# A two-layer graph attention kernel: weight loads tied to ScalarE during the scores, a reordered softmax at the end of a pass, and block stores moved to the second superblock

## The chip, the cores and the metric

The kernel runs on one core of one Trainium2 chip. The metric is the device time of one execution in microseconds (us); the figure given for a kernel is the median of several executions. A core has a matrix engine (TensorE, PE in the profile), three engines for element-wise work (VectorE, DVE; ScalarE, ACT; GpSimd, POOL) and a queue engine (SyncE, SP) that issues nearly all transfers here. Every engine runs its own instructions in order and waits for the others by semaphores.

## The reference, cut to what matters

The input is x, 128 graphs of 64 nodes with 768 features, and a symmetric adjacency of zeros and ones for each graph. A layer norm and a rectifier give h; two graph attention layers follow; x is added at the end.

```python
h = jnp.maximum(_layernorm(x, axis=-1), 0.0)
for l in range(L):                                             # L = 2
    m_left  = jnp.einsum('bsh,oh->bso', h, W_left[l])
    m_right = jnp.einsum('bsh,oh->bso', h, W_right[l])
    u_left  = jnp.einsum('bih,bjh->bij', h, m_left) / temper
    u_right = jnp.einsum('bih,bjh->bij', h, m_right) / temper
    u = u_left * adj_tri + u_left * diag_mask + u_right * jnp.swapaxes(adj_tri, 1, 2)
    delta_exp_u = jnp.exp(u) * adj
    attention = delta_exp_u / (jnp.sum(delta_exp_u, axis=2, keepdims=True) + 1e-10)
    h_lin = jnp.einsum('bsh,oh->bso', h, W_lin[l]) + b_lin[l]
    h = jax.nn.relu(_layer_norm(jnp.matmul(attention, h_lin), ln_a[l], ln_b[l]))
return x + h
```

All arithmetic is in float32.

## The kernel before, in words

The graphs are cut into 16 blocks of 8 graphs (512 tokens), and for the first half of the work two blocks make a superblock: U = 0 to 7, of which U = 1 is "superblock two". Each layer has two passes.

**Pass one** (`pass_one`) computes, per superblock, the two projections `m_left` and `m_right` and, one superblock later, the scores and the softmax. The projections are not done as plain matrix products: the features are taken in three pairs of 128, and sums and differences of weight blocks (`W_OPS`) and of token blocks (`X_OPS`) turn the products into 29 smaller ones (`PRODUCTS`, NP = 29). `project` runs them: for product i, and for left and right (k = 0, 1), four calls of the matmul at line 522 into one of the PSUM banks X, Y, Z (left), V, `right` (right), and then `read`, in which ScalarE (line 303) or VectorE (line 221) adds a finished bank to the results `m`. At two fixed places, after products 0 and 2, `scores` (line 464) is put into the stream: 96 small matmuls for the first and for the second block of the superblock before. Each shows in the trace as 192 matmuls and as many weight loads of the array.

Order is written out by hand. A superblock has SLOTS = 116 slots, four to a product; `put(slot, f)` puts a piece of work there and `run(slot)`, called inside the loop over products, issues it; `idle` holds work that fills slots with nothing planned. So what stands in an engine's queue, and in which order, follows from slots, and each engine then waits only for what its instructions need.

**Weights.** In the first superblock of layer 0 (`first`) the sums of weights are computed on the way and each finished pair is stored to memory (`ws`, line 194). From then on `streamed` brings the pairs back: a ring of RINGS = 8 buffers `wp`, one 512 KB load per product (`stream`, line 197), sent by `done(i)`, which is called after product i:

```python
            HELD = {NP - 2: 1, NP - 1: 2, 0: 3, 1: 4}
                    while sent[0] < min(U * NP + i + RINGS - HELD.get(i, 0), NU * NP):
```

Without HELD, the load for product i + 7 is put into SP's queue after product i. With it, the loads that would stand around the two `scores` come later in the queue, all after product 2. The load itself waits only until the product that last used its buffer is finished on TensorE, wherever it stands in the queue.

**Tokens and h.** In layer 0, `load_rows` (line 368) brings a block's rows, `transpose_rows` computes mean and variance (line 338), the scale (394 to 396), the norm (399, ScalarE) and the transposes (414, VectorE), and `store` (410) puts the block's h into memory (`KEPT`, 1.5 MB); `load_h` (373) brings it back to the buffers `ht` when its turn comes. `block` places these steps in a superblock for the two blocks of the next one, from the slots in `starts`. Blocks 0 and 1 are made inside `first`, and their h is stored at slots 54 and 58 of superblock one (line 675) for use in pass two.

**Softmax.** `chain(u)` is a generator: masks (473, GpSimd), then as steps of `softmax(u)` the masked scores (480, two steps), their sum (484), the exponential (486, ScalarE), product and row sum (488, 490), division (492 to 494), a transpose (498) and eight small stores (504). Inside the pass these steps lie in slots. For the last two blocks, NB - 2 and NB - 1, they stand at the end of `pass_one`, lines 762 to 768, after their scores, with a part put into slots of pass two.

**Pass two** (`pass_two`) computes the third projection in `linear` (15 products of a similar scheme, line 1038, each read out by `read`), the product with the attention (`context`), the norm and the output. The bank X is set ahead of the first product by `fresh` (line 812); product 0 and product 2 both use bank X, so ScalarE must have read it between the two.

Of the kernel before, what the change touches and what calls it, by code (L numbers as in the profile page):

```python
# [17 lines left out]
def kernel(  # L18
# [12 lines left out]
    nc = tc.nc  # L31
# [25 lines left out]
    RINGS = 8  # L57
# [5 lines left out]
    none = [None]  # L63

    def put(slot, *fs):
        plan.setdefault(slot, []).extend(fs)

    def put_all(slot, fs, step=1):
        for f in fs:
            if f is not None:  # L70
                put(slot, f)
            slot += step
        return slot
# [50 lines left out]
    NP = len(PRODUCTS)  # L124
# [10 lines left out]
    RING = [wpool.tile([P, 2, K2, D], F32, name=f"wp{i}") for i in range(RINGS)]  # L135
# [4 lines left out]
    def room(n, m):  # L140
        return ROOM[:, n * K2 * D:(n + m) * K2 * D]
# [54 lines left out]
    def stream(l, n):  # L196
        nc.sync.dma_start(RING[n % RINGS], WS[l][n % NP])
# [34 lines left out]
    HT, TS = {}, {}  # L232
# [42 lines left out]
    def token_op(l, U, op, eng):  # L275
        i, o, sign, a, b = op
        t = new_ts((l, U, o))
        added(eng, t, sign, tokens(l, U, a), tokens(l, U, b))
        TS.setdefault((l, U), {})[o] = t

    AHEAD_X = 4
    SLOTS = 4 * NP

    def put_token_ops(l, U, part):

        count = {}
        for op in X_OPS:
            n = count[op[0]] = count.get(op[0], 0) + 1
            slot = 4 * (op[0] - AHEAD_X) + n - 1
            if (slot < 0) == (part == "before"):  # L290
                put(slot + (SLOTS if slot < 0 else 0), lambda op=op: token_op(l, U, op, nc.gpsimd))
# [20 lines left out]
    KEPT = [[dram.tile([P, C, T], F32, name=f"h{l}_{u}") for u in range(NB)] for l in range(L)]  # L312
# [4 lines left out]
    eps_in = const.tile([P, 1], F32, name="eps_in")  # L317
# [28 lines left out]
    def new_ht():  # L346
        turns.rotate(-1)
        return big.tile([P, C, T], F32, name=f"ht{turns[-1]}", bufs=1)
# [6 lines left out]
    def blocks_tile(pool):  # L355
        if pool is not None:
            return pool.tile([P, H // 32, Q, 32], F32, name="xb", bufs=1)
        return room(6, 6).rearrange("p (b q j) -> p b q j", q=Q, j=32)

    def load_rows(l, u, pool=None):  # L360

        XR[l, u] = []
        for g in range(2):
            t = rows_tile(pool, g)
            for a in range(4):
                i = 4 * g + a
                src = x[u * NBB + i] if l == 0 else ROWS[u][i]
                nc.sync.dma_start(t[a * 32:(a + 1) * 32], src.rearrange("(k j) h -> j k h", k=2))
            XR[l, u].extend([t[:, 0, :], t[:, 1, :]])
# [14 lines left out]
    def transpose_rows(l, u, pool=None):  # L384

        xr, todo = XR[l, u], []
        if l == 0:
            mv = stat.tile([P, Q, 2], F32, name="mv0", bufs=2)
            sd = stat.tile([P, Q], F32, name="sd0", bufs=2)
            rs = stat.tile([P, Q], F32, name="rs0", bufs=2)  # L390
            nb = stat.tile([P, Q], F32, name="nb0", bufs=2)

            def scale():
                nc.scalar.activation(sd, mv[:, :, 1], AF.Sqrt, bias=eps_in)
                nc.vector.reciprocal(rs, sd)
                nc.vector.scalar_tensor_tensor(nb, mv[:, :, 0], -1.0, rs, op0=ALU.mult, op1=ALU.mult)

            def norm(q):
                nc.scalar.activation(xr[q], xr[q], AF.Relu, bias=nb[:, q:q + 1], scale=rs[:, q:q + 1])

            norms = [lambda q=q: norm(q) for q in range(Q)]
            stats = [lambda q=q: mean_var(mv[:, q, :], [xr[q][:, :HH], xr[q][:, HH:]]) for q in range(Q)]
            for f in stats + none * (4 * (u < 4)) + [scale] + norms:
                todo.extend([f] + none * (u >= 4))
        xb = blocks_tile(pool)

        def store():
            to = KEPT[l][u].rearrange("(b i) c t -> i c b t", b=4)
            for a in range(4):
                nc.sync.dma_start(to[:, :, :, a * P:(a + 1) * P],  # L410
                                  xb[a * 32:(a + 1) * 32].rearrange("i (c b) q j -> i c b (q j)", b=4))

        for q in range(Q):
            todo.append(lambda q=q: nc.vector.transpose(
                xb[:, :, q, :], xr[q].rearrange("p (b j) -> p b j", j=32)))
            todo.extend(none * (l or u >= 4))
        todo.append(store)
        return todo
# [7 lines left out]
    def pass_one(l, aside):  # L426
        with (tc.tile_pool(name=f"ps_one{l}", bufs=1, space=bass.MemoryType.PSUM) as ps,
# [76 lines left out]
                        nc.sync.dma_start(to[a // 2, a % 2, g], at[a * 32:(a + 1) * 32, g])  # L504

            TURNS = {0: 0, 2: 1}
            HELD = {NP - 2: 1, NP - 1: 2, 0: 3, 1: 4}
            sent = [RINGS - 1 if l else NP + 5]

            def project(U, weights, done):  # L510
# [35 lines left out]
            def streamed(U):  # L546
                def done(i):
                    while sent[0] < min(U * NP + i + RINGS - HELD.get(i, 0), NU * NP):
                        stream(l, sent[0])
                        sent[0] += 1  # L550
                return (lambda i, k: RING[(U * NP + i) % RINGS][:, k]), done

            def first():
# [47 lines left out]
                hts = [new_ht() for _ in range(2)]  # L601
# [66 lines left out]
                for n, (s0, s1, s2, s3) in {4: (3, 4, 5, 8), 5: (6, 7, 8, 12), 6: (13, 14, 15, 19),  # L668
# [2 lines left out]
                    put(s1, lambda n=n: inverse(n))  # L671
                    put(s2, lambda n=n: norm(n))
                    put(s3, lambda n=n: turn(n), lambda n=n: settle(n))
                for n, slot in ((0, 54), (1, 58)):
                    put(slot, lambda n=n: nc.sync.dma_start(KEPT[0][n], hts[n]))
                put(3, lambda: load_rows(0, 2))
                count = {}
                for op in X_OPS:
                    n = count[op[0]] = count.get(op[0], 0) + 1
# [28 lines left out]
            for U in range(NU):  # L708
                if U:
                    weights, done = streamed(U)  # L710
                if l or U:
                    put_token_ops(l, U, "after")
                if U + 1 < NU:
                    def block(n, slot):
                        u = 2 * U + 2 + n
                        *todo, store = transpose_rows(l, u)
                        slot = put_all(slot, todo)
                        put(slot + 6, store)
                        if u + 1 < NB:
                            put(slot + 7, lambda: load_rows(l, u + 1))  # L720
                        slot = max(slot + 15, (92, 103)[n]) if U == 0 and l == 0 else slot + 15
                        put(slot, lambda: load_h(1, l, u))
                        if l:
                            put_all(slot + 20, affine(1, l, u))

                    if l:
                        starts = (6 if U else 20, 48)
                    else:
                        starts = (6, 52) if U else (26, 66)
                    for n, slot in enumerate(starts):  # L730
                        put(slot - 1, lambda n=n, slot=slot: block(n, slot))
                    if U:
                        for n in range(2):
                            steps = softmax(2 * U - 2 + n)
                            slot = put_all(20 + 40 * n if l else (34, 76)[n], steps[:6], 2)
                            slot = put_all(slot, steps[6:] + [lambda n=n: load_adj(2 * U + n)])
                            put(slot + 11, masked(2 * U + n))
                    else:
                        for n in range(2):
                            put((40 if l else 106) + 2 * n, masked(n))  # L740
                    put_token_ops(l, U + 1, "before")
                else:
                    for n in range(2):
                        put(12 + 28 * n, lambda n=n: load_h(2, l, n))
                        put_all(38 + 28 * n, affine(2, l, n))
                    for n in range(2):
                        steps = softmax(2 * U - 2 + n)
                        put_all(put_all(14 + 28 * n, steps[:6], 2), steps[6:])
                    put(40, lambda: load_adj(2 * U))
                    put(54, masked(2 * U))  # L750
                    put(SLOTS - 24, lambda: load_adj(2 * U + 1))
                    put(SLOTS - 10, masked(2 * U + 1))
                    put_sums_t((2, l, 0), 94, 2, 85)
                if U in aside:
                    aside[U]()
                project(U, weights, done)
                assert not plan, sorted(plan)
# [5 lines left out]
            scores(NB - 2, both[0])  # L763
            scores(NB - 1, ps_st.tile([P, 2 * TH], F32, name="Z"))
            one, two = softmax(NB - 2), softmax(NB - 1)
            for f in one[:2] + two[:2] + one[2:] + two[2:4]:
                f()
            put_all(2, two[4:])

    rows = {}  # L770

# [406 lines left out]
```

## Time and profile before

| | |
|---|---|
| median of 3 executions | 2746.46 us (2743.89 to 2749.26) |
| profiled execution | 2748.58 us |
| its span, first to last instruction | 2746.8 us |
| TensorE busy | 2689.4 us, 98% |
| VectorE, ScalarE, GpSimd busy | 54%, 30%, 50% |
| transfers | 567.81 MB, mean 207 GB/s |

Busy time is an average over stages. TensorE is busy nearly throughout, so what matters is where it is idle, and what it waits for there. In the lines of the profile, "out<-in xcount" names the buffers, the bracket at the end of a timeline row holds the idle time of the engine before it and what ended it, and "issue" is a wait for nothing that the profile shows. PE stands for the matmul, PEld for the load of the array's weights, L522 for line 522.

### The profile page before, as it was taken

The page shows a single profiled execution, that of the slowest core. Times are in us where ns is not written, and L with a number is a line of the kernel's source. Part 1 is how long each engine was busy: PE and PEld are TensorE (multiplying, and loading weights), DVE is VectorE, ACT ScalarE, POOL GpSimd, SP SyncE. Part 2 cuts the span into 40 slices and gives each one's busy share as a digit, 9 for nine tenths or more (in the row PEclk, how much of TensorE's full clock was granted, in tenths as well). Part 3 has the DMA queues.
Part 4 walks back from the last instruction along what each step waited for, and adds up shares of the span by engine and source line. Part 5 has one row for each costly group of instructions (what it writes and reads, how often), then busy time and mean ns, then how long its engine had stood idle before and what let it go on. Part 6 is the DMA issues. An engine that isn't in the chain of part 4 may idle for free.

```text
span 2746.8 us, 47294 instructions
## 1 busy us (share of the span) xinstructions
PE 2689.4 (98%) x18514; PEld 2309.1 (84%) x18514; DVE 1494.6 (54%) x2458; ACT 828.0 (30%) x1601; POOL 1380.5 (50%) x1071
## 2 busy tenths in 40 slices
PE   8899999999999999999999999999999999999998
PEld 7788888888888788888788888888888888888886
DVE  7745755647557433334333645545446475676667
ACT  4031231321310145445631221211212303444443
POOL 5534244333345766576343324335234185887886
PEclk9999999999999999999999999999999999999999
DMA  7967867768665334657586967868759524555655
GB/s 252 314 225 226 256 218 259 227 202 274 213 226 191 105 127 149 205 155 232 186 279 204 301 196 231 267 188 272 227 186 293 202 76 125 163 168 167 172 164 148
DMA packets 310222, 567.81 MB, mean 207 GB/s; under 512 B 62832, under 2 KB 190064, under 8 KB 301808
## 3 DMA queue, kind: packets, MB, share of 16 engines
q1 hardware_dynamic: 309840, 564.39, 64.7%
q8 instruction: 148, 2.42, 0.4%
q14 instruction: 74, 0.61, 0.1%
q10 hardware_dynamic: 160, 0.39, 0.0%
HBM read 429.40 MB, written 135.27 MB: 206 GB/s over the span
## 4 chain that ended last, share of the span: by engine, by line
PE 93%; POOL 2%; DVE 2%; issue 1%; DMA 1%; ACT 0%; DVEq 0%; POOLq 0%; ACTq 0%; SPq 0%
PE right L522 17%; PE X L1038 12%; PE X L522 10%; PE V L522 10%; PE Y L522 9%; PE Z L522 9%; PE V L1038 8%; PE Y L1038 6%; PE both L464 4%; PE Z L1038 4%; PE aux L846 2%; POOL room L221 1%; PE aux L869 1%; POOL ts L221 1%; PE Y L869 0%
## 5 line engine op out<-in xcount | busy, mean ns | idle before, releaser
L221 POOL TENSOR_TENSOR ts<-ht 128x512 f32<-128x512 f32 x352 | 478.7, 1366 | 176.5 <-PE X L1038 76.8
L221 POOL TENSOR_TENSOR ts<-ht,ts 128x512 f32<-128x512 f32 x192 | 253.2, 1327 | 386.4 <-PE V L522 232.7
L522 PE MATMUL right<-ts,wp 128*128 128x252 f32 (+1 forms) x1632 | 382.1, 377 | 0.0
L522 PEld LDWEIGHTS right<-ts,wp 128*128 128x128 f32 x1632 | 311.1, 191 | 39.1
L473 POOL TENSOR_TENSOR wm<-adj,tri 128x256 f32<-128x256 f32 x60 | 42.8, 736 | 433.0 <-DMA wp<-ws 285.4
L221 DVE TENSOR_TENSOR m<-m,X 128x512 f32<-128x512 f32 x160 | 105.5, 684 | 282.9 <-ACT m L303 199.8
L1038 PE MATMUL X<-room,ts 128*128 128x256 f32 x1024 | 247.2, 383 | 10.1 <-ACT hl L303 9.9
L221 DVE TENSOR_TENSOR m<-m,right 128x504 f32<-128x504 f32 (+1 forms) x304 | 199.2, 672 | 90.3 <-PE right L522 77.1
L522 PE MATMUL Z<-ts,wp 128*128 128x256 f32 x992 | 234.5, 379 | 0.0
L221 POOL TENSOR_TENSOR ts<-ht,ht 128x512 f32<-128x512 f32 x128 | 163.3, 1286 | 138.8 <-PE right L522 93.6
L1038 PEld LDWEIGHTS X<-room,ts 128*128 128x128 f32 x1024 | 193.3, 192 | 42.8 <-issue 12.5
L522 PE MATMUL X<-ts,wp 128*128 128x256 f32 x872 | 208.7, 382 | 1.0 <-DVE wp L221 1.0
L522 PEld LDWEIGHTS Z<-ts,wp 128*128 128x128 f32 x992 | 188.4, 190 | 24.9
L522 PE MATMUL V<-ts,wp 128*128 128x252 f32 (+1 forms) x864 | 201.6, 376 | 0.0
L303 ACT ACTIVATE m<-right 128x504 f32<-128x504 f32 (+1 forms) x64 | 36.1, 590 | 546.7 <-PE both L464 526.7
L522 PEld LDWEIGHTS X<-ts,wp 128*128 128x128 f32 x872 | 165.3, 191 | 24.9 <-issue 1.6
L1038 PE MATMUL Y<-room,ts 128*128 128x256 f32 x768 | 183.6, 381 | 0.0
L522 PEld LDWEIGHTS V<-ts,wp 128*128 128x128 f32 x864 | 164.2, 190 | 20.4
L380 ACT ACTIVATE ht<-ht,b_col,a_col 128x512 f32<-128x512 f32 x192 | 140.8, 803 | 112.6 <-DMA ht<-h 112.6
L1038 PEld LDWEIGHTS Y<-room,ts 128*128 128x128 f32 x768 | 146.9, 191 | 20.9 <-issue 0.6
L221 DVE TENSOR_TENSOR m<-m,Y 128x512 f32<-128x512 f32 x144 | 95.7, 683 | 118.6 <-PE Y L522 107.4
L221 DVE TENSOR_TENSOR hl<-hl,V 128x512 f32<-128x512 f32 (+1 forms) x136 | 89.0, 655 | 129.1 <-PE V L1038 121.5
(221 smaller groups left out, 4866.6 us busy)
## 6 DMA issues: line engine op xcount, KB each, us to landing
wp<-ws SPq DMA_DIRECT2D x435, 512.0 KB, 5.4
ht<-h SPq DMA_DIRECT2D x62, 1536.0 KB, 8.8
h<-room SPq DMA_DIRECT2D x112, 384.0 KB, 6.2
z<-z SPq DMA_DIRECT2D x128, 192.0 KB, 3.1
ws<-wp SPq DMA_DIRECT2D x93, 256.0 KB, 4.3
xr<-in_x_dram SPq DMA_DIRECT2D x120, 192.0 KB, 3.7
out_dram<-xr SPq DMA_DIRECT2D x120, 192.0 KB, 2.6
room<-in_x_dram SPq DMA_DIRECT2D x112, 192.0 KB, 5.2
```

Of the source, the lines that this page charges most:

```text
L221: (eng.tensor_add if sign == "+" else eng.tensor_sub)(o, a, b)
L303: nc.scalar.activation(to(o), p, AF.Copy, scale=1.0 if sign == "+" else -1.0)
L380: nc.scalar.activation(ht, ht, AF.Relu, bias=cols[1][:, c:c + 1], scale=cols[0][:, c:c + 1])
L464: nc.tensor.matmul(p[h * S + e:h * S + e + 32, q, e:e + 95], ht[:, c, b * S + e:b * S + e + 32], mb[:, e:e + 95], start=(c == 0), stop=(c ...
L473: nc.gpsimd.tensor_tensor(wm[:, :, k], adj[:, :, 1 - k], tri[:, k].unsqueeze(1).to_broadcast([P, Q, S]), op=ALU.mult)
L522: nc.tensor.matmul(p[:, g], wk[:, c, g * P:(g + 1) * P], tk[:, c, :].rearrange("p (b s) -> p b s", s=S)[:, :, :ns], start=(new and g == c ...
L846: nc.tensor.matmul(cx[k][i, m, :HH], at[j, q, :], hl[j, q, m * HH:(m + 1) * HH], start=True, stop=True)
L869: nc.tensor.matmul(parts[r, k][n][i], at[j, q, :], hl[j, q, cut], start=True, stop=True)
L1038: nc.tensor.matmul(p[:, n], b[t][:, c, r * P:(r + 1) * P], w[s][:, c, :], start=(i in FIRST and i not in PRELOAD and n == c == 0), stop=(c ...
```

## The change

Four edits, in `transpose_rows`, `pass_one` and the functions in it.

1. HELD is shortened: product 27 no longer holds a load back, so the load for product 5 of the next superblock goes to the queue there, and the load for product 6 and the three after it are sent after product 2. The first of them, in all superblocks but the first of each layer, is preceded by a ScalarE copy of one column into its buffer, so that the load also waits for that copy, and the copy stands in ScalarE's order behind the reads that follow the second `scores`.
2. At the end of pass one, the sum and the exponential of block NB - 2 go ahead of the masked scores of block NB - 1, and all further steps of block NB - 1 go to slots from 3 on in pass two.
3. The stores of h for blocks 0 and 1 go from slots 54 and 58 of superblock one to slots 20 and 26 of superblock two; the row load for block 4 goes from the end of block 3's work (slot 90) to slot 112.
4. In layer 0 the work on a superblock's blocks begins at slots 26 and 62 in superblock one (26 and 66 before) and at 8 and 52 later (6 and 52 before), and blocks 2 and 3 get two empty slots between norm and transposes.

```diff
@@ transpose_rows
             for f in stats + none * (4 * (u < 4)) + [scale] + norms:
                 todo.extend([f] + none * (u >= 4))
+            todo.extend(none * (2 * (u < 4)))
@@ pass_one
-            HELD = {NP - 2: 1, NP - 1: 2, 0: 3, 1: 4}
+            HELD = {NP - 1: 1, 0: 2, 1: 3}
@@ streamed
                     while sent[0] < min(U * NP + i + RINGS - HELD.get(i, 0), NU * NP):
-                        stream(l, sent[0])
+                        if U and i == 2 and sent[0] == U * NP + RINGS - 2:
+                            nc.scalar.copy(RING[sent[0] % RINGS][:, 0, 0, :1], eps_in)
+                            stream(l, sent[0])
+                        else:
+                            stream(l, sent[0])
                         sent[0] += 1
@@ first
-                for n, slot in ((0, 54), (1, 58)):
-                    put(slot, lambda n=n: nc.sync.dma_start(KEPT[0][n], hts[n]))
@@ the loop over superblocks
+                if l == 0 and U == 1:
+                    for n in range(2):
+                        put(20 + 6 * n, lambda n=n: nc.sync.dma_start(KEPT[0][n], HT[1, 0, n]))
...
                         if u + 1 < NB:
-                            put(slot + 7, lambda: load_rows(l, u + 1))
+                            put(SLOTS - 4 if U == 0 and l == 0 and n else slot + 7, lambda: load_rows(l, u + 1))
...
-                        starts = (6, 52) if U else (26, 66)
+                        starts = (8, 52) if U else (26, 62)
@@ the end of pass_one
             one, two = softmax(NB - 2), softmax(NB - 1)
-            for f in one[:2] + two[:2] + one[2:] + two[2:4]:
+            for f in one[:4] + two[:2] + one[4:]:
                 f()
-            put_all(2, two[4:])
+            put_all(3, two[2:])
```

## The prediction

> **What bounds the kernel now.** I read the page first: shares of busy time and the queues.
>
> ```profile
> PE 2689.4 (98%) x18514; PEld 2309.1 (84%) x18514; DVE 1494.6 (54%) x2458; ACT 828.0 (30%) x1601; POOL 1380.5 (50%) x1071
> ...
> q8 instruction: 148, 2.42, 0.4%
> ```
>
> TensorE sets the time; no matmul is added or removed, so only its idle time (2746.8 - 2689.4 = 57.4 us) and its slow restarts can move. The second line says that TensorE's own instructions come by DMA in 148 pieces of 16 KB. Next the waits of TensorE, longest first (us in total, times, longest):
>
> ```profile
> PE both L464 <- issue: 13.0, 9, 2.8
> PE X L1038 <- ACT hl L303: 9.9, 2, 5.1
> PE Y L522 <- DMA wp<-ws: 6.3, 1, 6.3
> PE Y L522 <- DVE room L221: 3.4, 1, 3.4
> PE Z L522 <- issue: 2.8, 1, 2.8
> ```
>
> These five are 35.4 us. The timeline places each. One stall inside a scores run:
>
> ```profile
> 250.64 4.12 PE L464 MATMUL both<-m,ht 128*32 128x95 f32 x188
> ...
> 250.74 0.32 SPq L197 DMA_DIRECT2D wp<-ws  x1
> ...
> 255.41 0.36 PE L464 MATMUL both<-m,ht 128*32 128x95 f32 x4 [0.66 <-issue]
> ```
>
> Four matmuls from its end the run stops with nothing to wait for but instructions; a 512 KB weight load was issued 0.1 us after its start. How traffic matters, by window (length, TensorE, load, VectorE, ScalarE, GpSimd, clock, DMA share, GB/s):
>
> ```profile
> 686.60:694.20 7.60, 4.79 (x195) 4.40 (x195) 2.56 (x9) 1.08 (x2) 7.44 (x7) 1.00 0.78 281
> 902.70:911.50 8.80, 8.33 (x385) 7.96 (x384) 3.48 (x6) 0.39 (x1) 8.72 (x8) 1.00 0.03 6
> ```
>
> At 281 GB/s one run of scores loses 2.81 us; at 6 GB/s two runs together lose 0.47. Then the end of layer 0's pass one, ScalarE and TensorE:
>
> ```profile
> 914.06 1.97 PE L1038 MATMUL Z<-room,ts 128*128 128x256 f32 x8 [0.56 <-DVE wp L480]
> 920.86 3.22 PE L1038 MATMUL X<-room,ts 128*128 128x256 f32 x8 [4.83 <-ACT hl L303]
> 923.87 2.37 PE L1038 MATMUL Y<-room,ts 128*128 128x256 f32 x8
> ```
> ```profile
> 915.04 0.42 ACT L486 ACTIVATE adj<-adj 128x256 f32<-128x256 f32 x1 [11.95 <-DVE adj L484]
> 919.81 0.42 ACT L486 ACTIVATE wp<-wp 128x256 f32<-128x256 f32 x1 [4.35 <-DVE wp L145]
> 920.13 0.58 ACT L303 ACTIVATE hl<-X 128x512 f32<-128x512 f32 x1
> ```
>
> The read of X stands behind the last block's exponential, which stands behind the whole softmax of the block before. And the start of superblock two:
>
> ```profile
> 132.41 3.75 PE L522 MATMUL Y<-ht,wp 128*128 128x256 f32 x8 [6.26 <-DMA wp<-ws]
> 135.96 2.06 PE L522 MATMUL right<-ht,wp 128*128 128x252 f32 x8
> ```
>
> [...] 148 x 256 = 37888 against about 37900 in the program. The stalls come at most once a run, 1.3 to 1.5 us after a piece has passed. [...] at 281 GB/s no piece passed in the 4.1 us of that run. [...] after 3.44 us idle eight matmuls took 3.75 us, after 2.81 us none were slower (usual: 1.89).
>
> **The change, part by part.** The order of TensorE's instructions, and so where its pieces begin, is unchanged.
>
> *Weights held back (14 superblocks).* Before, the "held" loads wait only for their ring slot: one is issued 3.4 us before each scores run and one 0.1 us into it. After, load 5 (load n brings the weights of product n) goes at its usual time, 10 us before, and load 6 waits for a one-column ScalarE copy that stands behind the four reads of `right` and `Z` that wait for the second scores; everything later on SP's queue waits behind it. Both runs lie clear of weight loads. Working of a stall: a piece is asked for some 50 instructions ahead (the 902 us window), so a run of 21 ns per pair uses a 256-instruction piece and that lead in 3.23 us. Without traffic pieces followed each other 3.6 us apart there: 3.65 - 3.23 = about 0.4, I take 0.45 a stall. The nine stalls that I let shrink stand in the waits as 13.0 - 2.8 + 2.8 = 13.0, plus 9 x 0.22 hidden by modelled ends (245 ns against 21), plus 1.85 slow restart at 2157.95: 16.9. After: 9 x 0.45 = 4.0. Gain 12.9 (bounds: 0 if the load is innocent, 15). The tenth (141.4 us, 2.78) I leave, since new traffic meets it.
>
> The copies: 14 x 0.3 us (the row of one-column activations, 294 ns) on an engine 30% busy; the next read of X ended 0.75 us before the bank is rewritten (377.37 against 378.12), so 0. What is late next: load 6 issues 6.5 us after the second scores start (reads end 376.87 - 370.63 = 6.2), lands 3.7 to 5.8 later (first weights of the bursts at 795.98, 2137.88, 685.06), so at 10.2 to 12.3; product 6 starts at 4.06 + 3 x 3.43 = 14.35. Slack 2 to 4 us: 0. Loads 7 to 9 land 1.3 to 1.9 us apart, wanted 3.43 apart. In the last superblocks the 1.5 MB h load and w_lin loads also fall behind them: still ahead of use.
>
> *Softmax tail (both layers).* Sum and exponential of the last block but one go ahead of the last block's masks, under its scores (4 us of matmuls hide them), and the last block's rest moves to slots 3 to 15 of pass two. The first read of X then follows its product: product 2 starts at 914.06 + 1.97 = 916.0, not 920.86. VectorE: masks end 913.9, the softmax rest 4.0, a read 0.7, the sum 0.4, the exponential on ScalarE 0.5: 919.6; the next read of X to 920.2, against product 4 at 919.9: a new wait of 0.4. Product 4 starts at 920.3 instead of 926.07: 5.8. Layer 1 in the same way 2268.0 instead of 2274.2 (a new wait of 0.9): 6.2. Sum 12.0. Cover gone, it costs the 4.8 and 5.1 again.
>
> *Block stores, rows.* Two 1.5 MB h stores leave the first superblock (10 us each in flight), and the 1.5 MB row load for block 4 moves from about slot 90 to 112. SP is then at the loads of h and of the first ring weights some 7 to 8 us earlier (113.91 and 123.17 now), so superblock two starts without its wait: 6.26 + 2.2 slow restart (5.81 against 3.62 for the product) = 8.4. The row load now runs under the first scores of superblock two: the reason that I leave that stall. The stores land behind load 10 in superblock two, 3 MB where 3.4 us per 0.5 MB load leave half the queue free: 0.
>
> *First superblock's spacing.* Two transposes move behind the sum that TensorE awaits at 61.96: idle 3.44 falls to about 1.7 and the restart (3.2) goes, then 1.8 is lost to the right half's sums: 2.9 ahead. But the rows of block 3 are issued 2.9 us later (the store before them waits for later transposes) and their statistics stand 4 slots earlier: VectorE blocks from 75 to 79 and again to 82, the sum for product 18 ends at 85.9, where it is now (85.6). Net 0; bounds -5 to +4. From superblock two on, layer 0's first block starts two slots (1.7 us) later; its h is loaded at slot 49 and first read at slot 112, so 0; without that cover VectorE would be late by the 1.7 us.
>
> Sum: 12.9 + 12.0 + 8.4 = 33.3. The profiled execution took 2748.6 (span 2746.8): 2715.3. It lies 2.1 above the median of the three runs, so I expect 2714 there.
>
> **Rivals.** (1) The load is innocent: pieces are late because a scores run eats them too fast; for it, 0.47 and 0.94 us of stalls at both tails without traffic; against it, 2.8 against 0.7 with and without much traffic. Gain 20.4: 2726. (2) The first superblock gets worse: VectorE, in order, sits at block 3's statistics while TensorE goes cold; 5 to 8 us back: 2720. (3) Slower: the tie starves TensorE. If load 6 lands x us after product 6 is due, 14 x is lost in 14 superblocks; it decides from (33.3 + 5.5) / 14 = 2.8 us, a landing 10.7 us after issue. The 1.5 MB transfers took that long in the first superblock (10.2), 512 KB loads 8.9 there at most; at 4 us late it gives 2714 + 14 x 4 = 2770. (4) The tie doesn't hold anything: the copy's place in ScalarE's order, behind reads that wait for scores, excludes it nearly; it equals (1).
>
> **How the numbers follow.** All three gains 0.62 (own range 2706 to 2722); (1) with (4) 0.18; (2) 0.12; (3) 0.05; none of it visible 0.03. 0.2% is 5.5 us, about what a measurement tells from no change. Faster 0.92, same 0.03, slower 0.05. Range 2703 to 2732: down by a larger gain in the first superblock, up past (1).
>
> **What would show it.** Right: no ScalarE wait at L1038 above 1 us; superblock two's first product without a DMA wait; scores' issue waits under 6 us; weights issued in fives some 6.5 us into the second scores. Wrong: TensorE waiting for `wp<-ws` at each superblock's product 6, idle time at product 18, or scores stalls of the old size with clear queues.

## The result, and the profile after

The kernel after takes 2719.43 us (median; 2718.93 to 2720.2), the kernel before 2747.14 us on the same chip. The ratio is 0.99 with a 95% interval of 0.9883 to 0.9918: 27.7 us less, where 33.3 were predicted (2714, range 2703 to 2732). The profiled executions lie 29.1 us apart (2748.58 and 2719.48), and so do their spans; the places below are read from them.

First line of the page of after, then TensorE's waits, longest first (us in total, times, longest):

```profile
PE 2681.2 (99%) x18514; PEld 2302.4 (85%) x18514; DVE 1503.8 (55%) x2458; ACT 829.7 (31%) x1615; POOL 1381.4 (51%) x1071
```
```profile
PE both L465 <- issue: 3.9, 4, 2.9
PE Z L523 <- DVE ht L221: 2.2, 1, 2.2
PE Y L523 <- DVE ht L186: 2.1, 1, 2.1
PE right L523 <- DVE m L221: 2.0, 2, 1.6
PE Y L523 <- DVE room L221: 1.7, 1, 1.7
PE X L1044 <- ACT hl L303: 1.7, 2, 1.2
...
PE Y L523 <- DMA wp<-ws: 1.2, 1, 1.2
```

The stalls for instructions fell from 13.0 to 3.9 us, the reads of X by ScalarE from 9.9 to 1.7, the wait for weights at superblock two from 6.3 to 1.2. New are the second to fourth lines: 6.3 us of waits for VectorE, all in superblock one, where two older ones of 2.2 us are gone. (Lines 464, 522 and 1038 of before are 465, 523 and 1044 here.)

The same points of the program in both timelines, us from the start, show where the time went:

| point | before | after | ahead |
|---|---|---|---|
| product 12 of superblock one | 61.96 | 60.34 | 1.6 |
| product 20 of superblock one | 95.07 | 97.33 | -2.3 |
| product 0 of superblock two | 132.41 | 129.58 | 2.8 |
| its first scores | 137.95 | 133.17 | 4.8 |
| its second scores | 152.18 | 149.16 | 3.02 |
| last scores, layer 0 | 902.72 | 892.57 | 10.15 |
| pass two, product 4, layer 0 | 926.07 | 910.43 | 15.64 |
| last scores, layer 1 | 2249.15 | 2226.99 | 22.16 |
| pass two, product 4, layer 1 | 2274.23 | 2245.11 | 29.12 |

The start (edits 3 and 4) gave 3.0; the scores of the two layers 7.13 and 6.52, together 13.7; the tails, which are the ends of pass one, 5.49 and 6.96, together 12.5.

The windows over a first scores run (the counterpart of the one at 686.60) and over the last two runs of layer 0: length, TensorE, load, VectorE, ScalarE, GpSimd, clock, DMA share, GB/s.

```profile
679.41:687.01 7.60, 7.60 (x209) 7.05 (x209) 2.62 (x9) 1.08 (x2) 7.44 (x7) 1.00 0.04 10
892.55:901.35 8.80, 8.46 (x386) 8.10 (x386) 4.40 (x7) 0.80 (x2) 8.72 (x8) 1.00 0.02 6
```

In 7.60 us the first has 7.60 of matmuls where it had 4.79, with 10 GB/s beside it where there were 281. The end of pass one in layer 0, TensorE and ScalarE:

```profile
905.57 1.89 PE L1044 MATMUL X<-room,ts 128*128 128x256 f32 x8
907.30 1.89 PE L1044 MATMUL Y<-room,ts 128*128 128x256 f32 x8
910.43 1.97 PE L1044 MATMUL X<-room,ht 128*128 128x256 f32 x8 [1.24 <-ACT hl L303]
...
909.38 0.42 ACT L487 ACTIVATE wp<-wp 128x256 f32<-128x256 f32 x1 [3.01 <-DVE wp L485]
909.71 0.58 ACT L303 ACTIVATE hl<-X 128x512 f32<-128x512 f32 x1
```

The second X follows its predecessor at once (4.83 us idle before). Only the third waits, behind the last block's exponential. And the start of superblock two:

```profile
129.58 1.96 PE L523 MATMUL Y<-ht,wp 128*128 128x256 f32 x8 [1.17 <-DMA wp<-ws]
...
133.17 3.45 PE L465 MATMUL both<-m,ht 128*32 128x95 f32 x154
139.52 1.22 PE L465 MATMUL both<-m,ht 128*32 128x95 f32 x38 [2.90 <-issue]
140.67 3.43 PE L523 MATMUL Z<-ht,wp 128*128 128x256 f32 x8
```

Its weights are nearly in time, and there is no slow restart at its first product (1.96 against 3.75). But the first scores stop after 154 of 192 matmuls, and the product behind them runs at half clock (3.43; the trace gives a granted clock of 0.50 there). By the start of the product after them, that run costs 5.0 us more than an undisturbed one, where it cost 3.2 before:

```profile
137.95 3.46 PE L464 MATMUL both<-m,ht 128*32 128x95 f32 x154
144.18 1.02 PE L464 MATMUL both<-m,ht 128*32 128x95 f32 x38 [2.78 <-issue]
145.13 1.99 PE L522 MATMUL Z<-ht,wp 128*128 128x256 f32 x8
```

The stop itself is nearly as long there (2.78 against 2.90 us); most of the difference is the half clock behind it.

### The profile page after: what moved, and what is told of

Its sections match the earlier page's. It is cut to its first block, busy times and chain, and to the rows that moved or that the text cites. A ratio compares the mean times of both kernels' runs of the same rounds, so it can differ in the third digit from the quotient of the medians.

```text
span 2717.7 us, 47304 instructions
## 1 busy us (share of the span) xinstructions
PE 2681.2 (99%) x18514; PEld 2302.4 (85%) x18514; DVE 1503.8 (55%) x2458; ACT 829.7 (31%) x1615; POOL 1381.4 (51%) x1071
## 3 DMA queue, kind: packets, MB, share of 16 engines
q8 instruction: 148, 2.42, 0.4%
## 4 chain that ended last, share of the span: by engine, by line
PE 93%; DVE 2%; DMA 1%; SPq 1%; issue 0%; ACT 0%; DVEq 0%
PE right L523 17%; PE X L1044 12%; PE X L523 11%; PE V L523 10%; PE Z L523 9%; PE Y L523 9%; PE V L1044 8%; PE Y L1044 6%; PE both L465 5%; PE Z L1044 4%; PE aux L852 2%; PE aux L875 1%; PE Y L875 0%; DMA wp<-ws 0%; DVE m L221 0%
## 5 line engine op out<-in xcount | busy, mean ns | idle before, releaser
L1010 POOL TENSOR_TENSOR z<-z,b 128x768 f32<-128x768 f32 x62 | 112.7, 1831 | 89.7 <-DVE z L1007 89.7
```

What stands on the lines that cost most here:

```text
L1010: nc.gpsimd.tensor_add(zs[k], zs[k], rows["b"])
```

## The experiments

Theory A: three separate gains that add up (the tie, which is the ScalarE copy that load 6 must wait for, with the shorter HELD; the tails; the start), and a scores run stalls where a border between two 16 KB pieces of TensorE's instructions falls in it while data moves. Rivals are named with the runs. "Loses" below is the time of a scores run above 4.06 us, slower products behind it counted in; an undisturbed run reads 0.1.

### Edit 2 alone: the softmax order

The kernel before with

```diff
-            for f in one[:2] + two[:2] + one[2:] + two[2:4]:
+            for f in one[:4] + two[:2] + one[4:]:
...
-            put_all(2, two[4:])
+            put_all(3, two[2:])
```

> The kernel before with edit 2 alone (the softmax order at the end of both passes one). By places in the trace of after, the two tails gave 5.5 and 7.0 us. Theory A (three separate gains that add up): 12.5 us below the kernel before, about 2734.5; the waits of X on ScalarE fall from 4.83 and 5.1 us to about 1.2 and 0.4; scores runs stall as before (about 13 us of issue waits). Rival B (the tails gained only because other edits moved work away from them, or what the scores seem to gain is a part of it): a gain under 8 or over 17 us.

Measured: 2734.67 us against 2747.57 before, ratio 0.9954 (0.9939 to 0.9968): 12.9 less. Two lines of its waits:

```profile
PE both L464 <- issue: 11.1, 8, 2.5
...
PE X L1038 <- ACT hl L303: 1.0, 2, 0.7
```

The ScalarE waits fall from 9.9 to 1.0 us and the stalls stay. The tails gain by themselves what they gain in after.

### Edit 1 alone: HELD and the tie

The kernel before with

```diff
-            HELD = {NP - 2: 1, NP - 1: 2, 0: 3, 1: 4}
+            HELD = {NP - 1: 1, 0: 2, 1: 3}
...
+                        if U and i == 2 and sent[0] == U * NP + RINGS - 2:
+                            nc.scalar.copy(RING[sent[0] % RINGS][:, 0, 0, :1], eps_in)
+                            stream(l, sent[0])
```

> The kernel before with edit 1 alone (HELD shortened and load 6 tied to a ScalarE copy). Theory A (weight loads under the scores delay the instruction pieces): 13 to 14 us below the kernel before, about 2733.5; every scores run but those of superblock two's start loses under 1 us; ScalarE's waits at both tails stay 4.8 and 5.1 us. Rival C (the load is innocent, a scores run simply outruns its pieces): under 2 us of gain, stalls of 1 to 3 us at the same scores runs as before. Rival D (the tie starves TensorE): waits for wp<-ws at product 6 of the superblocks.

Measured: 2734.01 us, ratio 0.9951 (0.9934 to 0.9967): 13.6 less.

```profile
PE X L1042 <- ACT hl L303: 10.7, 2, 5.5
...
PE both L464 <- issue: 3.5, 3, 2.8
```

The stalls fall to 3.5 us, of which 2.8 is the one at superblock two's start, and TensorE nowhere waits for weights at a product 6. Rivals C and D fall.

### Edits 3 and 4 alone: the start

The kernel after with the lines of edits 1 and 2 put back.

> The kernel before with edits 3 and 4 alone (stores of h and row load moved, spacing of the first superblock). Theory A: about 3 us below the kernel before, about 2744, as the trace of after shows at the second scores of superblock two: the first product of superblock two waits some 1.2 us for its weights where it waited 6.3, but product 20 of superblock one starts 2 us later than before and the first scores of superblock two stall about 5 us. Prediction on record: 8.4 us for these edits, about 2738.5.

Measured: 2747.53 us over 12 runs against 2747.57 over 15, ratio 0.9999 (0.999 to 1.0008): no gain that can be seen, at most 2.7 us. Its profile is 2.2 us below that of the kernel before (spans 2744.6 and 2746.8); there too product 20 starts at 97.18, superblock two's first product waits 1.82, and its first scores lose 5.0. The three parts sum to 12.9 + 13.6 + 0.0 = 26.5; together they gave 27.7.

### After without the copy

The kernel after with

```diff
-                        if U and i == 2 and sent[0] == U * NP + RINGS - 2:
-                            nc.scalar.copy(RING[sent[0] % RINGS][:, 0, 0, :1], eps_in)
-                            stream(l, sent[0])
-                        else:
-                            stream(l, sent[0])
+                        stream(l, sent[0])
```

> The kernel after without the one-column ScalarE copy; HELD stays shortened, so the place of every load in the queue is that of after, and only the wait is gone. Theory A (the tie is what keeps the loads out of the scores): 11 to 13 us above after, about 2731, with 0.5 MB moved in the first 4 us of each scores run and stalls of 0.7 to 4.7 us at the runs that had them in the kernel before. Rival E (the shorter HELD does it alone, the copy holds nothing): within 2 us of after, about 2719.

Measured: 2733.6 us, ratio 0.9952 (0.9937 to 0.9966): about 14 us of the gain are gone. The timeline over the same first scores that the prediction showed:

```profile
250.65 4.11 PE L465 MATMUL both<-m,ht 128*32 128x95 f32 x188
...
250.75 0.32 SPq L197 DMA_DIRECT2D wp<-ws  x1
256.20 0.14 PEld L465 LDWEIGHTS both<-m,ht 128*32 128x32 f32 x4 [1.65 <-issue]
256.20 0.36 PE L465 MATMUL both<-m,ht 128*32 128x95 f32 x4 [1.44 <-issue]
```

The load is back 0.1 us into the run, and so is the stall. Without one 0.21 us copy on ScalarE per superblock nothing of edit 1's gain is left; rival E falls. In after the copy and the loads behind it stand well clear of the second scores at 257.60 to 261.66:

```profile
263.71 0.21 ACT L551 COPY wp<-eps_in 128x1 f32<-128x1 f32 x1
...
263.95 8.61 SPq L197 DMA_DIRECT2D wp<-ws  x8
```

### The border of the pieces, moved

The kernel before with

```diff
-                for _ in range(34):
+                for _ in range(98):
                     nc.tensor.transpose(p[:, :P], KEEP["ident"], KEEP["ident"])
```

> The kernel before with 64 more warm-up transposes at the start of TensorE's stream: 128 more instructions, so that every 16 KB piece begins half a piece earlier in the program; the warm-up adds about 7 us, everything else is unchanged, the weight loads too. Theory A (a stall comes where a piece border falls in the second quarter of a scores run, and traffic makes it long): other scores runs stall. Counting the runs after superblock one in order (layer 0: superblock two first, second, ...): stalls of 0.5 us and more at superblock three's second and four's first of layer 0, at superblocks six and seven's second or first, and in layer 1 at superblocks two and three and at six and seven's neighbours, and none at the runs near 250, 478, 576, 588, 1814 and 2150 us of the kernel before. Rival G (traffic alone decides, the border's place doesn't matter): the same scores runs stall, by about the same amounts.

Measured: one execution, 2753.09 us. Its TensorE timeline:

```profile
142.96 4.13 PE L464 MATMUL both<-m,ht 128*32 128x95 f32 x192
...
265.76 1.02 PE L464 MATMUL both<-m,ht 128*32 128x95 f32 x38 [0.36 <-issue]
...
364.32 1.01 PE L464 MATMUL both<-m,ht 128*32 128x95 f32 x35 [1.43 <-issue]
...
377.62 0.36 PE L464 MATMUL both<-m,ht 128*32 128x95 f32 x4 [1.19 <-issue]
```

The scores runs inside the passes that stalled before are all clean here, among them the first of superblock two, with 1.6 MB moving in its first 4 us as before; eleven others stall. (My list in words was right for layer 1 and wrong in part for layer 0: it named three, four, six and seven, and the stalls lie in three, four, five, seven and eight.)

How to count it: a line "x154" followed by "x38" is a stop after 154 pairs of load and matmul, so 308 instructions. Counting TensorE's instructions in the trace (two for each matmul, one for each semaphore instruction) in pieces of 256 (about 37900 instructions in before, 148 packets of 16 KB on queue q8), with one origin for all kernels, set so that the stop in superblock two's first run is a border, puts the two borders of that run at instructions 53 and 309 before, and the borders of the runs at 261.95, 359.43 and 372.31 here at 53 and 309, 59 and 315, 120 and 376. They stop after 154, 157 and 188 pairs: 308, 314, 376. All three stop at their second border. Of the ten stops inside the passes in before, nine do so too; in the tenth (686.64) that border lies just behind the run's end, and the stop comes in the next product (2.81 us). The count gives eleven runs with a first border between 53 and 132, and these are the eleven.

That it is the instructions that come late shows in the traces of before and after: each stop at a border inside the passes, ten and nine of them, ends 1.2 to 1.5 us after a packet of an instruction piece has passed (queue q8; 142.77 and 144.18 before, 138.20 and 139.52 in after). Rival G falls, with one correction of my own picture: traffic alone does nothing (142.96; and four runs of before without such a border, with 312 to 392 GB/s in their first 4 us, lose 0.1), and borders almost without traffic cost at most 0.9 us (after, 4 to 14 GB/s in the first 4 us of these runs). TensorE's issue waits at the scores are 13.1 us where they were 13.0: moving the borders alone gains nothing here.

### Edit 4 undone

The kernel after with

```diff
-            todo.extend(none * (2 * (u < 4)))
...
-                        starts = (8, 52) if U else (26, 62)
+                        starts = (6, 52) if U else (26, 66)
```

> The kernel after with edit 4 undone (starts 26, 66 and 6, 52; no empty slots between norm and transposes); stores, row load at slot 112, tie and tails as in after. Theory A (edit 4 costs VectorE waits in the first superblock): product 12 late again (idle 3.4 us at about 62), but product 20 of superblock one starts at 92.4 to 95.1 as in the three runs with the old spacing, not at 97.2 to 97.3; 2 to 5 us below after, about 2716. Rival F (edit 4 gains what it was priced at or more, and the row load is what delays the first superblock): product 20 no earlier than 97, 0 to 3 us above after.

Measured: 2716.95 us (2715.25 to 2718.87), ratio to the kernel before 0.9884 (0.9867 to 0.99). After, run beside it, took 2720.38 (2716.32 to 2723.74), ratio 0.9898 (0.9883 to 0.9912). So 3.4 us less in the medians, but the ranges overlap. The trace is clearer: product 20 starts at 95.80, just outside my 92.4 to 95.1 and earlier than in after and its repetition (97.3 and 97.7), superblock two's second scores at 147.83 (149.16 and 152.25). VectorE in after shows what edit 4 did there, with TensorE's product 18:

```profile
81.16 1.02 DVE L338 BATCH_NORM_STATS2 st<-room 128x6 f32<-128x384 f32 x2 [5.00 <-DMA room<-in_x_dram]
...
86.45 0.68 DVE L221 TENSOR_TENSOR ht<-wp,ht 128x512 f32<-128x512 f32 x1
...
87.28 1.97 PE L523 MATMUL Z<-ts,ht 128*128 128x256 f32 x8 [2.22 <-DVE ht L221]
```

VectorE stands 5 us at block 3's statistics, whose rows are not there, and the sum for product 18 and the reads of banks stand behind them. With the edit undone the statistics begin at 82.74, without any wait.

### The row load moved past the scores

The kernel after with the row load of block 4 in superblock two, its blocks later there, and the starts of before in superblock one:

```diff
-                        if u + 1 < NB:
-                            put(SLOTS - 4 if U == 0 and l == 0 and n else slot + 7, lambda: load_rows(l, u + 1))
+                        if u + 1 < NB and not (U == 0 and l == 0 and n):
+                            put(slot + 7, lambda: load_rows(l, u + 1))
...
                 if l == 0 and U == 1:
+                    put(13, lambda: load_rows(0, 4))
...
-                        starts = (8, 52) if U else (26, 62)
+                        starts = (8, 52) if U > 1 else (22, 64) if U else (26, 66)
```

> The kernel after with the row load for block 4 moved out of superblock one, to slot 13 of superblock two (after its scores), blocks 4 and 5 started at slots 22 and 64 there, and blocks 2 and 3 at 26 and 66 as before (the two empty slots stay). Theory A (the 1.5 MB row load under the first scores of superblock two makes their stall as long as it is, and block 3's statistics four slots earlier make VectorE late): the first scores lose 2 us or less where they lost 5.0, product 20 starts at 93 to 95: 4 to 6 us below after, about 2714. Rival H (the weight stores and the first five weight loads suffice for that stall): it stays at 4 to 5 us, 0 to 3 us below after.

Measured: 2739.11 us, ratio 0.9962 (0.9949 to 0.9975), 19 us above after beside it. The first scores of superblock two still lose 4.6: without the row load, the weight stores and five weight loads move 1.6 MB in their first 4 us. Rival H was right on the stall, and nobody on the total. Product 12 starts at 60.56 and product 20 at 94.36: the two empty slots, which stayed, give the early product 12 without the loss at product 20, so of edit 4 it is the start of block 3's work at slot 62 instead of 66 that costs. Two places of its timeline:

```profile
176.91 2.76 PE L523 MATMUL V<-ht,wp 128*128 128x252 f32 x8 [3.62 <-ACT m L303]
...
258.53 4.11 PE L465 MATMUL both<-m,ht 128*32 128x95 f32 x188
265.49 0.36 PE L465 MATMUL both<-m,ht 128*32 128x95 f32 x4 [2.85 <-issue]
267.38 2.90 PE L523 MATMUL Z<-ht,wp 128*128 128x256 f32 x6 [1.52 <-DMA ht<-h]
```

The rows queue behind the tied weights, so ScalarE waits 5.6 us for the statistics behind its square root, with the read of bank V behind that. The blocks end later, and the 1.5 MB load of h now falls under the next first scores, with a border in them: that run loses 7.9 instead of 0.5 to 0.8, 1.5 of it in a wait for that h. Between the two, TensorE waits 4.2 us for a sum on GpSimd (product at 215.63).

### After once more

> The kernel after once more, unchanged, beside the three others on the same chip: about 28 us below the kernel before, 2719; product 20 of superblock one at 97 to 97.5, the first scores of superblock two 4.5 to 5 us longer than normal.

Measured: 2720.38 us. The first scores of superblock two lose 6.3 here and lost 5.0 in the first profile. The stop is the same (2.94 and 2.90 us idle), but what stands behind it is slower: the last 38 matmuls of the run took 1.81 us, the two products after it 3.78 and 2.27, and in the first profile 1.22, 3.43 and 1.86.

### Filling the wait at product 12

TensorE waits there for a sum anyway. 28 small matmuls shift all later borders by 112 instructions. They were put into the kernel with edit 4 undone, and into after:

```diff
+                def fill():
+                    for _ in range(28):
+                        nc.tensor.matmul(both[0][:32, :95], KEEP["ident"][:, :32], KEEP["ident"][:, :95],
+                                         start=True, stop=True)
+
+                put(47, fill)
```

> The kernel of the run with edit 4 undone (stores, row load, tie and tails as in after; 2716.95 us), and 28 small matmuls on the identity, whose result nobody reads, in TensorE's stream between products 11 and 12 of superblock one, where TensorE waits 3.4 us for a sum. 28 matmuls are 112 instructions: every later piece begins 112 instructions earlier in the program, and no border falls in the stalling part of the first or second scores of superblock two. Theory A (a stall needs a border in a scores run, traffic sets its length): the first scores of superblock two lose under 0.3 us although 1.4 MB still move under them (3.4 us there without the fill); the wait at 62 us falls to 2.2 us and the slow restart goes; 4 to 6 us less, about 2712. Rival G (traffic alone decides): the stall of 3.4 to 5 us stays, 2715.5.

> The kernel after with the same 28 matmuls at the same place, where TensorE waits 1.7 us there. Theory A: the first scores of superblock two lose under 0.3 us where they lost 5.0 and 6.3; 4 to 6 us below after, about 2714.5. Rival G: as after, 2719 to 2720.

Measured: 2716.25 us (2714.96 to 2716.93), ratio 0.9883 (0.9868 to 0.9897), and 2717.54 (2714.44 to 2719.08), ratio 0.9887 (0.9872 to 0.9901). The first of the two:

```profile
58.70 4.76 PE L682 MATMUL both<-ident 128*32 128x95 f32 x56
...
132.30 2.31 PE L464 MATMUL both<-m,ht 128*32 128x95 f32 x98
135.79 2.16 PE L464 MATMUL both<-m,ht 128*32 128x95 f32 x94 [1.19 <-issue]
```

The stall went where the border went: the count puts it at instruction 197, and the run stops after 98 pairs. It loses 1.6 and 2.0 us instead of 3.4 to 6.3; the stop itself is 1.19 and 1.54 us instead of 2.9, and no slow product follows (1.99 in both). That is less than I expected to gain: one border in the middle of these two runs still stalled them under this traffic. And the fill itself took 4.76 us, more than the wait it was put in. Neither total is clear of the same kernel's without the fill.

The control is the first of these with

```diff
-                    for _ in range(28):
+                    for _ in range(64):
```

> The control of the fill: the kernel with edit 4 undone and 64 small matmuls at that place, 256 instructions, one whole piece, so that every later border falls where it fell without them. Theory A: the first scores of superblock two stall again, 3 to 6 us; the slow restart goes, since TensorE is idle 0.7 us there only; about 1 us below the run without the fill, 2716. Rival I (the fill helps by keeping TensorE at full clock or by its delay, and the borders are innocent): no stall there, about 2712.

Measured: 2722.35 us, ratio 0.9905 (0.9888 to 0.9921); 5.4 above the run without a fill, which was made on another chip: the 128 matmuls took 10.64 us in a wait of 3.4, and the second scores of superblock two start 4.5 us later (152.36 against 147.83). For the question it was made for, the answer is plain: with the borders a whole piece further, the run stops after 154 pairs again and loses 3.5. Rival I falls.

```profile
144.37 1.02 PE L464 MATMUL both<-m,ht 128*32 128x95 f32 x38 [3.05 <-issue]
```

### The fill in four column groups

The kernel with 28 matmuls and edit 4 undone, and

```diff
-                    for _ in range(28):
-                        nc.tensor.matmul(both[0][:32, :95], KEEP["ident"][:, :32], KEEP["ident"][:, :95],
+                    for n in range(28):
+                        nc.tensor.matmul(both[0][n % 4 * 32:n % 4 * 32 + 32, :95], KEEP["ident"][:, :32],
+                                         KEEP["ident"][:, :95],
```

> The run with 28 small matmuls and edit 4 undone once more, but the 28 go round the four groups of 32 columns of the array as those of the scores do, so that the fill (56 matmuls in the trace) should take about 1.2 us at 21 ns each, where it took 4.76 us at 83 ns in one group and itself delayed product 12 by 1.4 us. Theory A: the fill lies inside the wait for the sum; product 12 starts near 62.2 at full clock, the first scores of superblock two stall at the piece border inside them (after about 98 of 192) for 1 to 2 us as in the run before it: 1 to 1.5 us below that run, 2715. Rival: the fill's own time doesn't matter, because VectorE's waits at products 18 and 20 take the gain back: 2716.

Measured: 2715.43 us (2715.09 to 2716.27), ratio 0.9874 (0.9858 to 0.9891).

```profile
58.53 1.35 PE L682 MATMUL both<-ident 128*32 128x95 f32 x56
62.03 1.97 PE L522 MATMUL Y<-ts,room 128*128 128x256 f32 x8 [2.16 <-DVE room L221]
...
135.43 2.16 PE L464 MATMUL both<-m,ht 128*32 128x95 f32 x94 [1.79 <-issue]
```

Product 12 starts 1.4 us earlier than with the slow fill and is not slow (1.97 us), but product 20 only 0.2 earlier (94.18 and 94.42): VectorE takes it back, as the rival said. The first scores lose 2.2 us, a little over the 1 to 2 expected. 0.8 us less in the median is within the spread. It is the best kernel of the study: its four runs lie at 2715.1 to 2716.3, the eight runs of after, not made beside it, at 2716.3 to 2723.7. The intervals of the ratios overlap, so the 4 us between the medians are likely, not shown.

## Why the prediction was right, and where it was not

**Weights held back** (12.9 expected): right. 13.6 alone, 14 when only the copy is taken out, 13.7 by places. Load 6 is issued 6.35 us after the second scores start and lands at 9.6 (263.95 and 267.16 against 257.60; expected 6.5 and 10.2 to 12.3); product 6 starts at 272.04, 4.9 us later. The tie starves nobody (rival 3). The innocent load (rival 1) and the copy that holds nothing (rival 4) are refuted by the run with the copy taken out. What the prediction did not have is that here the border decides which runs stall at all (in before, ten of 28 inside the passes). It took the nine stalls as given, and since the change leaves TensorE's instructions as they are, that did no harm.

**Softmax tail** (12.0): right. 12.9 alone, 12.5 by places. The new wait in layer 0 is 1.24, not 0.4, and 0.43 in layer 1, not 0.9.

**Block stores, rows** (8.4): this is the step that failed, and it is nearly the whole miss. Together with the spacing it gave 3.0 by places and 0.0 in the medians when alone. "SP is at the loads of h and of the first ring weights some 7 to 8 us earlier" does not hold:

```profile
111.86 0.59 SPq L373 DMA_DIRECT2D ht<-h  x1
...
120.52 8.36 SPq L197 DMA_DIRECT2D wp<-ws  x5
```

They are issued 2.1 and 2.7 us earlier than before (113.91, 123.17). I had subtracted the row load's whole issue time. But the long issues, up to 1.9 us each, that had fallen on row loads fell on the weight stores queued behind block 3's stores instead. And the first ring weight goes out only when the first load of h, eight transfers ahead, has landed: at 120.45, 0.07 us before, as at 123.11 and 123.17 before. The h load was in flight 8.6 us instead of 9.2.

The sum of this part comes out so: from start to start the slow restart was worth 1.95 us and not 2.2, which leaves 8.2; 1.2 of it is the wait for weights that stayed, 1.8 was lost in the first scores and 2.3 by the spacing, and 3.0 remain. The last loss is in part hidden by the wait: the wait of product 0 fell by 5.1, but 2.3 of that only because product 28 ends later, and with edit 4 undone product 0 waits 2.96.

The 1.8 us lost in the first scores are hardly the row load's, which was the reason to "leave that stall": the first 4 us of that run move 1.6 MB before and 1.4 MB in after. TensorE stands idle 2.4 to 2.8 us there in the three kernels with before's row load (before, edits 1 and 2 alone) and 2.7 to 3.1 in six with the load at slot 112, so the load adds some 0.3 us at most (without it, 2.49). The rest is what followed the stop. In before, with edit 4 undone and in the control with 64 matmuls the next product took 1.99 us, and they lost 3.2 to 3.5; in the others it took 2.60 to 3.78 (3.43 in after, at a granted clock of 0.50), and they lost 4.5 to 6.3. The 3.2 was a lucky draw.

**First superblock's spacing** (0, between -5 and +4): inside its bounds, on the bad side, -2.3 at product 20. Up to product 12 it went as priced (idle 1.72 where 1.7 was forecast). After it VectorE waited 5.0 us for block 3's rows, and the sum for product 18 ended at 87.1 instead of 85.9. This is the front half of rival 2. Its other half, TensorE going cold, did not happen: after 2.2 us idle eight matmuls took 1.97. That was luck: after 1.96 us idle at the same product the run of after with 28 matmuls took 3.43. The result lies at rival 2's 2720 by this and by the weights that came early too little.

Of its signs of being right, two came: the scores' issue waits are 5.4 us (3.9, and 1.5 at the tails), and the weights are issued from 6.35 us into the second scores. Two came in part: a ScalarE wait of 1.24 us, where 1 was the limit, and 1.2 us of waiting for weights at superblock two. One sign of being wrong came too, the idle time at product 18. So the number is right because the two large terms were (13.7 and 12.5 by places), and the third, mis-sized, was the smallest.

## What to carry to other kernels

Here a wait for "issue" inside a dense run of small matmuls took two things, a border of an instruction piece and data on the queues (without such a border a run lost 0.1 us in before and after, with one but almost no data at most 0.9). Count the first, and clear the second, which here one cheap instruction (0.21 us) in the right engine's order did. A transfer taken off a queue gave back only what the next waiting one was short of: look for what else holds it (here an issue slot, and the landing of an older transfer) before its whole time is booked as a gain. A loss read from one profile is one draw: the half clock behind one stop here made the next product 1.44 us longer (3.43 against 1.99), with the stop itself only 0.12 longer.

## What the runs showed of the hardware

A run of scores goes at 21 ns per pair of load and matmul. In before and after, the count puts a first border between 53 and 132 in ten of the 28 runs inside the passes. In before these ten lost 0.7 to 2.0 us where 135 to 143 GB/s moved in their first 4 us, and 3.1 to 4.6 at 311 to 409 GB/s. In after nine of them lost 0.1 to 0.9 at 4 to 14 GB/s, and the first of superblock two 5.0 at 359. Half clock behind a stop is counted in (2150.59 before, 133.17 in after). The other eighteen lost 0.1 in both.

Small matmuls of 32 columns took 85 ns each when all went to one group of columns (56 in 4.76 us) and 24 ns when they went round four groups (56 in 1.35 us), 3.5 times faster.

The length of an idle time did not by itself tell whether a slow product would follow. At the first scores of superblock two, 2.42 to 2.94 us idle were followed by a product of 2.60 to 3.78 us in seven profiles, and 2.78, 2.94 and 3.05 us by one of 1.99 in three (before, edit 4 undone, the control with 64 matmuls). At product 12, 3.44 us idle were followed by 3.75 us before, by 3.43 with edit 2 alone, and by 1.97 with edit 1 alone. At product 18, 1.96 us were followed by 3.43 (after with 28 matmuls) and 2.22 by 1.97 (after). So the two places of before that the prediction went by, 3.44 us idle with a slow product behind it and 2.81 us without, drew no line between the two.

The granted clock was recorded at 0.50 for five stretches in the profile of before and for one in that of after (the last one of each, which runs past the kernel's end, left out). They lasted 3.41 or 6.83 us, and in the 3.41 us just ahead of each TensorE was idle for 2.7 to 3.4 us. Behind the stops at 141.40 and 691.18 of before, 2.78 and 2.81 us idle, it was recorded at 1.00.
